# A 3x3 convolution in column tiles: four products of 32 channels, one for each strip of seven image columns

## The chip, the cores and the metric

The kernel runs on one core of a Trainium2 chip. The metric is the device time of one execution in microseconds (us). A core has a matrix engine (TensorE, PE in the profile; PEld is its loading of weights), VectorE (DVE), ScalarE (ACT), GpSimd (POOL) and SyncE (SP), which here issues nearly all transfers. [...]

## The reference

The input is 32 images of 56 x 56 positions with 96 channels, fp32. Layer 0 is a block with a convolution:

```python
h = (x - mean) * rsqrt(var + eps) * ln_w + ln_b           # over the 96 channels
x1 = (einsum('bhwc,cd->bhwd', h, w_in) + b_in)[..., :192]
y = conv3x3(x1, conv_w, padding='SAME') + conv_b          # 192 -> 96 channels
x = x + silu(y)
```

Layer 1 takes the 3136 positions of an image as tokens. It adds a token mixer and then a feed-forward part, each after a normalisation over the channels:

```python
h = relu(bn1(einsum('bnc,hc->bnh', ln(t), w1)))           # 96 -> 192
X = fft(h, axis=1, norm='ortho')
xr = relu(X.real * rd - X.imag * id + rb)
xi = relu(X.imag * rd + X.real * id + ib)
t = t + bn2(einsum('bnh,ch->bnc', ifft(xr + 1j * xi).real, w2))
t = t + ffn(ln(t))                                        # 96 -> 384 -> 96, quantized
```

The values in the feed-forward part are rounded to an 8-bit float before each product.

## The kernel before

**Layout.** A token's number is 28 p + j. The partition p has 112 values (56 image rows, two halves of a row), and j is one of 28 columns in a half row. Tiles of tokens are [112, columns, 96]. LN_CHUNKS cuts the 28 columns into chunks of 8, 8, 8 and 4; a *group* g is four columns, and there are seven.

**Convolution.** w_in and the 3x3 weights are folded into one kernel when the program starts. In the direction of the rows it is done in a transformed form: `image` multiplies the normalised tokens (xa) by the table rows6. This gives, for each of 14 groups of four image rows, six sums of rows, with channels on partitions, in the tile img of [97, 2 halves, 30 columns, 6 sums, 14 groups]. There is one img for all images. `make_seam` copies the columns where the halves meet. `conv` then multiplies img with the weights wv: three *parts* with two of the six sums each, and for each sum three column offsets dx. `conv_sums`, `conv_row` and `conv_silu` turn the parts into four image rows (VectorE) and apply SiLU (ScalarE). `to_tokens` transposes the result back into tokens, and `conv_end` (L398) adds x from a tile of its own and starts the statistics of the next normalisation.

Before the change `conv` works on a chunk: a product has 97 input rows, 96 output channels and 2 x 8 x 14 = 224 columns (112 for the last chunk). An image has 4 x 3 x 6 = 72 of them. The profile shows each fp32 product as two passes.

**The token mixer.** `product_a` and `transform_a` (L209, L218) go through a table to the DRAM tile da; `forward` (L233) fetches it as at and makes px. Its third kind of step, u = 2, puts products of 64 columns into partitions 0 to 63 and 64 to 127 of px. `product_w2` and `inverse` (L272, L276, L286) lead to the DRAM tile de, and `transform_out` (L294) takes it back as y to the tokens. `ffn_tokens`, `ffn_in`, `ffn_relu` and `ffn_out` are the feed-forward part. `ffn_add` (L331, L332) writes the sum to a tile o, and `store` sends o to the output.

**Buffers.** Tiles of conv, image and to_tokens share one tag of PSUM with two buffers (tag q). Tokens t have three buffers for each chunk; x has two, o two. The working tiles m, sd and s have two each.

**Order.** The steps are put into a list with a time each: `plan(b)` gives steps of image b times in units of an eighth of an image, shifted by 8 for each image. CONV, FIRST, BACK and FFN are the times at which convolution, mixer, way back and feed-forward part begin. The list is sorted and the steps are called in that order. The framework then orders the instructions of each engine by its own timeline, with this list as priorities (`schedule_with_timeline_sim=True`), so a step's instructions needn't stay together. Steps of up to five images are under way at a time.

Of the kernel before, what the change touches and what calls it, by code (L numbers as in the profile page):

```python
# [38 lines left out]
F32 = mybir.dt.float32  # L39
# [6 lines left out]
C = 96  # L46
# [15 lines left out]
LN_CHUNKS = ((0, 8), (8, 16), (16, 24), (24, 28))  # L62


LN_W, LN_B, CONV_B, B_IN, BN1, BN2, NPAR = 0, 1, 2, 3, 5, 13, 17
# [15 lines left out]
def hybrid_kernel(ctx: ExitStack, tc: tile.TileContext, x, par, spar, w_in, conv_w, w1, w2, fw1, fb1, fw2, fb2, fa, fb, ib, ia, rows6, out):  # L81
# [18 lines left out]
    convb = par_sb[:, CONV_B : CONV_B + 1]  # L100
# [48 lines left out]
    def image(xa, n, b, j0):  # L149

        ps = psq.tile([C + 1, n, 2, WC * WG], F32, tag="q", name=f"im_{b}_{j0}")
        for j in range(n):
            nc.tensor.matmul(ps[:, j], xa[:, j, :], rows6_sb, start=True, stop=True)  # L153
        nc.scalar.copy(img[:, :, j0 + 1 : j0 + 1 + n].rearrange("c h j k g -> c j h (k g)"), ps)

    def conv(s, part, b, i):

        j0, j1 = LN_CHUNKS[i]
        n = j1 - j0
        ps = s[part] = psq.tile([C, 2, 2, n, WG], F32, tag="q", name=f"cv_{b}_{i}_{part}")  # L160
        for at, k in enumerate(PAIRS[part]):
            for dx in range(3):
                cols = img[:, :, j0 + dx : j1 + dx, k, :]
                nc.tensor.matmul(ps[:, at], wv[:, k, dx, :], cols, start=(dx == 0), stop=(dx == 2))  # L164
        if part == 0:
            m = s["m"] = work.tile([C, 2, 2, n, WG], F32, tag="m", name=f"m_{b}_{i}")
            nc.scalar.copy(m, s.pop(0))

    def conv_sums(s, b, i):

        j0, j1 = LN_CHUNKS[i]
        n = j1 - j0
        m, ps = s.pop("m"), s.pop(1)
        sd = s["sd"] = work.tile([C, 2, 2, 2, n, WG], F32, tag="sd", name=f"sd_{b}_{i}")
        nc.vector.tensor_tensor(sd[:, 0], m, ps, ALU.add)
        nc.vector.tensor_tensor(sd[:, 1], m, ps, ALU.subtract)
        s["y"] = work.tile([C, n, WG, 4, 2], F32, tag="s", name=f"s_{b}_{i}")
        conv_row(s, 1, 1, 2.0)
        conv_row(s, 2, 0, 4.0)

    def conv_row(s, r, at, scale):
        row = s["y"][:, :, :, r, :].rearrange("c j g h -> c h j g")
        nc.vector.scalar_tensor_tensor(row, s["sd"][:, at, 1], scale, s["sd"][:, at, 0], ALU.mult, ALU.add)

    def conv_silu(s):

        sd = s["sd"]
        nc.vector.tensor_tensor(sd[:, :, 0], s.pop(2), sd[:, :, 0], ALU.add)
        conv_row(s, 0, 0, 1.0)
        conv_row(s, 3, 1, 8.0)  # L190
        nc.scalar.activation(s["y"], s["y"], AF.Silu, bias=convb)

    def to_tokens(s, b, g):
        pt = psq.tile([N1, G4, C], F32, tag="q", name=f"st_{b}_{g}")
        for j in range(G4):
            nc.tensor.transpose(pt[:, j, :], s[:, j].rearrange("c r i h -> c (r i h)"), ident[:C, :C])  # L196
        return pt
# [131 lines left out]
    def ffn_add(y1, tg, o, b, g):  # L329
        y2 = work.tile([N1, G4, C], F16, tag="y2", name=f"y2_{b}_{g}")  # L330
        nc.vector.tensor_tensor(y2, y1, b2q, ALU.add)  # L331
        nc.vector.tensor_tensor(o, tg, y2, ALU.add)  # L332

    class Image:


        def __init__(self, b):
            self.b = b
            self.tokens = x[b].rearrange("(p j) c -> p j c", j=N2)
            self.result = out[b].rearrange("(p j) c -> p j c", j=N2)  # L340
            self.x, self.t, self.s, self.n2t, self.hq = {}, {}, {}, {}, {}
            self.u, self.at, self.gt, self.gw, self.held = {}, {}, {}, {}, {}
            self.xa, self.xc, self.rs, self.xl, self.y, self.norm = {}, {}, {}, {}, {}, {}

        def load(self, i):
            j0, j1 = LN_CHUNKS[i]
            self.t[i] = tpool.tile([N1, j1 - j0, C + 1], F32, tag=f"t{i}", name=f"t_{self.b}_{i}")
            self.x[i] = xpool.tile([N1, j1 - j0, C], F32, tag="x", name=f"x_{self.b}_{i}")
            nc.sync.dma_start(self.x[i], self.tokens[:, j0:j1, :])

        def group(self, g, tiles=None):
            return (tiles or self.t)[g // 2][:, g % 2 * G4 : (g % 2 + 1) * G4, :]
# [21 lines left out]
    def make_image(im, i, j, n):  # L374
        image(im.xa[i][:, j : j + n], n, im.b, LN_CHUNKS[i][0] + j)

# [5 lines left out]
    def conv_part(im, i, part):  # L382
        if part == 0:
            im.s[i] = {}
        conv(im.s[i], part, im.b, i)

    def conv_first(im, i):
        conv_sums(im.s[i], im.b, i)

    def conv_last(im, i):  # L390
        conv_silu(im.s[i])

    def conv_tokens(im, g):
        im.held["st", g] = to_tokens(im.s[g // 2]["y"][:, g % 2 * G4 :], im.b, g)

    def conv_end(im, g):

        nc.vector.tensor_tensor(im.group(g)[:, :, :C], im.held.pop(("st", g)), im.group(g, im.x), ALU.add)  # L398
        for i in ended(g):
            im.rs[i] = stats(im.t[i], "b", im.b, i)  # L400

    def deviation(im, i):

        _, var, rs = im.rs[i]
        nc.vector.tensor_tensor(im.t[i][:, :, C], var, rs, ALU.mult)
# [65 lines left out]
    def back_end(im, g):  # L471

        tg = im.group(g)[:, :, :C]
        nc.vector.tensor_tensor(tg, im.held.pop(("py", g)), tg, ALU.add)
        for i in ended(g):
            mu, _, rs = stats(im.t[i], "c", im.b, i)
            im.norm[i] = mu, None, rs

    def normal(im, g, j):

        i = g // 2
        if j == 0:
            im.xc[g] = xnp.tile([N1, G4, C], F32, tag="xn", name=f"xn_{im.b}_{g}")
        mu, _, rs = im.norm[i]
        xc = im.xc[g]
        for j in (j, j + 1):
            at = g % 2 * G4 + j
            nc.vector.tensor_scalar(xc[:, j], im.t[i][:, at, :C], mu[:, at : at + 1], rs[:, at : at + 1], ALU.subtract, ALU.mult)  # L488
# [15 lines left out]
    def ffn_end(im, g):  # L504
        o = im.held["o", g] = work.tile([N1, G4, C], F32, tag="o", name=f"o_{im.b}_{g}")
        ffn_add(im.held.pop(("y1", g)), im.group(g)[:, :, :C], o, im.b, g)

    def store(im, g):
        o = im.held.pop(("o", g))
        nc.sync.dma_start(im.result[:, g * G4 : (g + 1) * G4, :], o)  # L510
# [8 lines left out]
    def plan(b):  # L519
# [5 lines left out]
        for i, (j0, j1) in enumerate(LN_CHUNKS):  # L525
            last = i == len(LN_CHUNKS) - 1

            at = CONV - 8 + 2 * (i + 1)
            ats = (-0.95, -0.7) if last else (0.2, 0.5, 0.85) if i == 2 else (0.25, 1.0, 1.5)
            put(at + ats[0] - (2.5 if b else 12), fetch, i)  # L530
            put(at + ats[0] - 1.15, take_in, i)
            for part, j in enumerate(range(0, j1 - j0, 3)):
                put(at + ats[part], make_image, i, j, min(3, j1 - j0 - j))

            at = CONV + 2 * i
            put(at + 0.6, im_load, i)
            ats = (0, 0.35, 0.7) if last else (0, 0.5, 1.25)
            for part in range(3):
                put(at + ats[part], conv_part, i, part)
            put(at + ats[1] + 0.2, conv_first, i)  # L540
            put(at + ats[2] + 0.2, conv_last, i)
            for g, off in zip(range(j0 // G4, j1 // G4), (1.85, 2.75)):
                put(at + off, conv_tokens, g)
                put(at + off + 0.15, conv_end, g)
            put(FIRST + 2 * i - 0.75, deviation, i)
        put(CONV - 0.6, make_seam)
# [23 lines left out]
        for m, (p0, p1) in enumerate(UNITS):  # L570
            both = p1 - p0 > PG
            for at, u in ((0, 0), (0.62, 1), (1.25, 2)) if both else ((0, 0), (0.62, 2)):
                at += 2 * m
                put(at, second, m, u)
                put(at + 0.22, second_parts, m, u)
                put(at + 0.42, second_relus, m, u)
# [6 lines left out]
    def im_load(im, i):  # L583
        im.load(i)

    CONV, FIRST, BACK, FFN = -12.3, -8, 8.38, 10.85
# [14 lines left out]
    run(CONV - 0.1)  # L601

    with tc.tile_pool(name="setup", bufs=1) as sp, tc.tile_pool(
# [4 lines left out]
        nc.sync.dma_start(spar_sb, spar)  # L608
        win = sp.tile([C, H], F32, name="win")
# [118 lines left out]
    tpool = ctx.enter_context(tc.tile_pool(name="tpool", bufs=3))  # L728
    xpool = ctx.enter_context(tc.tile_pool(name="xpool", bufs=2))
# [8 lines left out]
def dft_tables():  # L738
# [58 lines left out]
    for g in range(WG):  # L797
        for i in range(6):
            r = 4 * g + i - 1
            if 0 <= r < HW:  # L800
                for h in range(2):
                    rows6[r, h, h, :, g] = sums[:, i]
    tables = fa.reshape(N1, 112), fb.reshape(112, -1), ib.reshape(114, NP, 112), ia, rows6.reshape(N1, -1)
# [48 lines left out]
```

## Time and profile before

| | |
|---|---|
| median of 3 runs | 3285.62 us (3276.33 to 3288.96) |
| profiled execution | 3286.24 us, its span 3284.5 us |
| busy: PE, PEld, DVE, ACT, POOL | 3178.5, 2732.7, 2527.3, 2202.5, 573.4 us |
| chain that ended last | PE 88%, DMA 7%, DVE 2% |
| convolution's passes (L164) | 4608, 22% of the chain |
| granted TensorE clock, mean | 0.985 |
| transfers | 355.45 MB in 334551 packets, 129304 of them under 512 bytes; main queue 37.7% of 16 engines |

The span is the time from the first instruction to the last. Busy shares are unions of instruction times[...]. The chain is followed back from the last instruction to what released it. An image takes some 102 us in the middle of the span.

### The profile page before, as it was taken

How to read it: one execution, taken by the hardware profiler on the slowest of the kernel's cores; microseconds unless marked ns; L12 is line 12 of the kernel's file. 1: busy time of each engine (PE TensorE's matmuls, PEld its weight loads, DVE VectorE, ACT ScalarE, POOL GpSimd, SP SyncE). 2: the span in 40 equal slices, each digit the busy share in tenths (PEclk: the TensorE clock that was granted, in tenths of full speed). 3: DMA queues.
4: the chain of work that ended last, by engine and by line, in shares of the span. 5: the costliest groups of instructions: out<-in, count | busy, mean ns of one | idle time of the engine just before them, and what ended most of it. 6: DMA issues, size and time to landing. Idle time of an engine off the chain costs nothing.

```text
span 3284.5 us, 66741 instructions
## 1 busy us (share of the span) xinstructions
PE 3178.5 (97%) x23701; PEld 2732.7 (83%) x23701; DVE 2527.3 (77%) x7829; ACT 2202.5 (67%) x5232; POOL 573.4 (17%) x397
## 2 busy tenths in 40 slices
PE   7999999999999999999999999999999999999997
PEld 6888888888888888888888888888888888888875
DVE  4558777777878777877877777777777778777787
ACT  2566666766766666766666766667767666666776
POOL 1211111111211111112111111111111111121111
PEclk8999999999999999999999999999999999999997
DMA  4343334434344333344333344343344333443341
GB/s 109 94 116 98 104 110 123 120 99 112 94 118 120 109 107 105 106 117 119 111 102 109 107 117 123 96 112 104 110 123 119 100 103 101 120 118 99 104 117 55
DMA packets 334551, 355.45 MB, mean 108 GB/s; under 512 B 129304, under 2 KB 287400, under 8 KB 333992
## 3 DMA queue, kind: packets, MB, share of 16 engines
q1 hardware_dynamic: 332210, 349.01, 37.7%
q8 instruction: 188, 3.08, 0.4%
q10 hardware_dynamic: 2008, 2.17, 0.2%
q14 instruction: 145, 1.19, 0.1%
HBM read 196.93 MB, written 154.14 MB: 107 GB/s over the span
## 4 chain that ended last, share of the span: by engine, by line
PE 88%; DMA 7%; DVE 2%; ACT 1%; issue 1%; SPq 1%; POOL 0%; ACTq 0%; DVEq 0%; POOLq 0%
PE cv L164 22%; PE px L233 9%; PE pa L218 9%; PE ph L209 9%; PE im L153 7%; PE pg L276 5%; PE pe L286 5%; PE tp_n L146 5%; PE pg L272 5%; PE py L294 5%; PE pf L305 4%; PE po L322 3%; DMA de<-es 2%; PE st L196 2%; DMA at<-da 2%; DMA y<-de 1%
## 5 line engine op out<-in xcount | busy, mean ns | idle before, releaser
L164 PE MATMUL cv<-img,wv 97*96 97x224 f32 (+1 forms) x4608 | 882.4, 332 | 0.2
L164 PEld LDWEIGHTS cv<-img,wv 97*96 97x96 f32 x4608 | 662.0, 164 | 93.2 <-issue 11.2
L138 POOL TENSOR_TENSOR rs_c<-var_c,mhalf 112x8 f32<-112x8 f32 (+1 forms) x128 | 195.0, 1523 | 1679.7 <-DVE var_a L136 868.9
L212 ACT ACTIVATE h<-ph,rs_b 112x192 f32<-112x192 f32 x896 | 332.3, 429 | 177.5 <-PE ph L209 176.2
L233 PEld LDWEIGHTS px<-fb_sb,at 112*64 112x64 f32 (+1 forms) x3584 | 324.7, 165 | 132.7 <-issue 48.9
L233 PE MATMUL px<-fb_sb,at 112*64 112x112 f32 (+3 forms) x3584 | 381.9, 274 | 35.1 <-DMA at<-da 34.1
L307 ACT CAST h<-pf 128x448 f16<-128x448 f32 x672 | 363.8, 541 | 67.8 <-PE pf L305 64.5
L209 PE MATMUL ph<-w1a,n2t 97*112 97x192 f32 x1792 | 373.7, 328 | 4.1 <-DVE sv L252 2.8
L218 PE MATMUL pa<-h,fa_sb 112*112 112x384 f32 x896 | 365.6, 490 | 0.0
L138 POOL TENSOR_TENSOR rs_b<-var_b,mhalf 112x8 f32<-112x8 f32 (+1 forms) x128 | 190.4, 1488 | 984.7 <-DVE var_a L136 552.1
L153 PE MATMUL im<-rows_sb,xa 112*97 112x168 f32 x1792 | 325.2, 312 | 11.0 <-DVE xa L372 9.8
L488 DVE TENSOR_SCALAR xn<-t,st_c,rs_c 112x96 f32<-112x96 f32 x896 | 232.2, 325 | 111.3 <-POOL rs_c L138 108.7
L249 DVE SCALAR_TENSOR_TENSOR sv<-px,spar_sb,av 128x224 f32<-128x224 f32 (+2 forms) x352 | 153.4, 436 | 200.2 <-ACT av L240 199.3
L209 PEld LDWEIGHTS ph<-w1a,n2t 97*112 97x112 f32 x1792 | 290.7, 177 | 17.4 <-DVE sv L252 3.3
L153 PEld LDWEIGHTS im<-rows_sb,xa 112*97 112x97 f32 x1792 | 268.0, 167 | 43.2 <-issue 14.7
L219 ACT COPY u<-pa 112x384 f32<-112x384 f32 x448 | 215.4, 481 | 120.8 <-PE pa L218 111.5
L316 DVE CAST hq<-h 128x448 fp8e5<-128x448 f16 x672 | 257.9, 384 | 11.3 <-ACT h L313 5.4
L315 DVE TENSOR_SCALAR h<-h,b1q 128x448 f16<-128x448 f16 x658 | 215.4, 327 | 59.2 <-ACT h L307 54.4
L305 PE MATMUL pf<-n3t,w1q 96*128 96x448 fp8e5 x672 | 243.8, 363 | 9.6 <-ACT h L307 8.8
L276 PE MATMUL pg<-w2x,gt 128*112 128x96 f32 (+1 forms) x1792 | 251.6, 261 | 0.0
L238 ACT ACTIVATE av<-px,spar_sb 128x224 f32<-128x224 f32 (+2 forms) x352 | 156.7, 445 | 135.3 <-PE px L233 132.5
L276 PEld LDWEIGHTS pg<-w2x,gt 128*112 128x112 f32 (+1 forms) x1792 | 242.7, 179 | 0.2
(115 smaller groups left out, 6148.1 us busy)
## 6 DMA issues: line engine op xcount, KB each, us to landing
da<-u SPq DMA_DIRECT2D x224, 336.0 KB, 3.4
at<-da SPq DMA_DIRECT2D x224, 336.0 KB, 4.7
de<-es SPq DMA_DIRECT2D x448, 84.0 KB, 2.2
y<-de SPq DMA_DIRECT2D x224, 168.0 KB, 2.8
out<-o SPq DMA_DIRECT2D x224, 168.0 KB, 2.4
xl<-in_x SPq DMA_DIRECT2D x96, 336.0 KB, 3.4
x<-in_x SPq DMA_DIRECT2D x96, 336.0 KB, 4.1
xl<-in_x SPq DMA_DIRECT2D x32, 168.0 KB, 2.3
```

The source lines that it names most:

```text
L138: nc.gpsimd.tensor_tensor(rs, var, mhalf[:, :n], ALU.pow)
L153: nc.tensor.matmul(ps[:, j], xa[:, j, :], rows6_sb, start=True, stop=True)
L164: nc.tensor.matmul(ps[:, at], wv[:, k, dx, :], cols, start=(dx == 0), stop=(dx == 2))
L209: nc.tensor.matmul(ph[:, j, :], n2t[:, 2 * j2 + j, :], w1a, start=True, stop=True)
L212: nc.scalar.activation(h[:, j], ph[:, j], AF.Relu, scale=rs[:, 2 * j2 + j : 2 * j2 + j + 1])
L218: nc.tensor.matmul(pa, fa_sb, h, start=True, stop=True)
L233: nc.tensor.matmul(px[rows, j], lhs, fb_sb[:, first(p) : first(p + 1)], start=True, stop=True)
L276: nc.tensor.matmul(pg[:, half, j, :], lhs, w2x, start=False, stop=True, skip_group_check=True)
L305: nc.tensor.matmul(pf, w1q[:, k * 128 : (k + 1) * 128], n3t, start=True, stop=True)
L307: nc.scalar.copy(h1, pf)
L316: nc.vector.tensor_copy(hq[:, k, :], h2, saturate=False)
L488: nc.vector.tensor_scalar(xc[:, j], im.t[i][:, at, :C], mu[:, at : at + 1], rs[:, at : at + 1], ALU.subtract, ALU.mult)
```

## The change

The convolution is cut by output channels and by columns instead of by chunks:

- Output channels come in three blocks r of 32 (NR, CB). The 28 columns come in four strips t of seven (NT, CT). For each block, part, sum and dx there are four products with 32 output channels and 2 x 7 x 14 = 196 columns, one for each strip. Their results lie in partitions 32 t to 32 t + 31 of one PSUM tile, so an image has 3 x 3 x 6 x 4 = 216 products, in nine parts of 24.
- The steps after the products work on [128, ...] tiles with 392 elements, three times an image instead of four.
- A transpose in `to_tokens` now turns a [128 = 4 strips x 32 channels, 112] piece, and gives one column of each strip. So tokens are held in ORDER (0, 7, 14, 21, 1, 8, ...): the input, the tables and the output are permuted to match outside the timed program.
- The convolution of a block needs all columns. `make_image` takes two columns at a time. All of the next image's columns are planned after the last part of this image, where before chunks of both alternated.
- x is loaded into t itself, in two halves of 16 and 12 columns (HALVES), and the convolution's result is added in place. The statistics of the next normalisation become a step of their own, `norm_b`. `ffn_add` adds in place too, and the output is stored from t. Tiles x and o are gone, and t has four buffers.
- CONV goes from -12.3 to -14.7 and BACK from 8.38 to 8.5; the first px of an image is planned 0.14 units later.

```diff
+NT, CT = 4, N2 // 4
+CB, NR = 32, 3
+HALVES = ((0, 4), (4, NG))
+ORDER = [CT * t + g for g in range(NG) for t in range(NT)]
...
-    def image(xa, n, b, j0):
-        ps = psq.tile([C + 1, n, 2, WC * WG], F32, tag="q", name=f"im_{b}_{j0}")
-        for j in range(n):
+    def image(xa, b, g, t0):
+        ps = psq.tile([C + 1, 2, 2, WC * WG], F32, tag="q", name=f"im_{b}_{g}_{t0}")
+        for j in range(2):
             nc.tensor.matmul(ps[:, j], xa[:, j, :], rows6_sb, start=True, stop=True)
-        nc.scalar.copy(img[:, :, j0 + 1 : j0 + 1 + n].rearrange("c h j k g -> c j h (k g)"), ps)
+        j0 = CT * t0 + g + 1
+        nc.scalar.copy(img[:, :, j0 : j0 + CT + 1 : CT].rearrange("c h j k g -> c j h (k g)"), ps)
...
-        ps = s[part] = psq.tile([C, 2, 2, n, WG], F32, tag="q", name=f"cv_{b}_{i}_{part}")
+        ps = s[part] = psq.tile([128, 2, 2, CT, WG], F32, tag="q", name=f"cv_{b}_{r}_{part}")
         for at, k in enumerate(PAIRS[part]):
             for dx in range(3):
-                cols = img[:, :, j0 + dx : j1 + dx, k, :]
-                nc.tensor.matmul(ps[:, at], wv[:, k, dx, :], cols, start=(dx == 0), stop=(dx == 2))
+                for t in range(NT):
+                    cols = img[:, :, CT * t + dx : CT * (t + 1) + dx, k, :]
+                    w = wv[:, k, dx, r * CB : (r + 1) * CB]
+                    nc.tensor.matmul(ps[t * CB : (t + 1) * CB, at], w, cols, start=(dx == 0), stop=(dx == 2))
...
-    def to_tokens(s, b, g):
-        pt = psq.tile([N1, G4, C], F32, tag="q", name=f"st_{b}_{g}")
-        for j in range(G4):
-            nc.tensor.transpose(pt[:, j, :], s[:, j].rearrange("c r i h -> c (r i h)"), ident[:C, :C])
+    def to_tokens(s, b, r, half):
+        g0, g1 = HALVES[half]
+        pt = psq.tile([N1, g1 - g0, 128], F32, tag="q", name=f"st_{b}_{r}_{half}")
+        for g in range(g0, g1):
+            nc.tensor.transpose(pt[:, g - g0, :], s[:, g].rearrange("c r i h -> c (r i h)"), ident)
...
-        nc.vector.tensor_tensor(o, tg, y2, ALU.add)
+        nc.vector.tensor_tensor(tg, tg, y2, ALU.add)
...
+        def load(self, half):
+            n = G4 * (HALVES[half][1] - HALVES[half][0])
+            self.t[half] = tpool.tile([N1, n, C + 1], F32, tag=f"t{half}", name=f"t_{self.b}_{half}")
+            j0 = G4 * HALVES[half][0]
+            nc.sync.dma_start(self.t[half][:, :, :C], self.tokens[:, j0 : j0 + n, :])
...
+    def conv_end(im, r, half):
+        t = im.t[half][:, :, r * CB : (r + 1) * CB]
+        st = im.held.pop(("st", r, half)).rearrange("p j (t c) -> p (j t) c", c=CB)
+        nc.vector.tensor_tensor(t, st, t, ALU.add)
+    def norm_b(im, i):
+        im.rs[i] = stats(im.chunk(i), "b", im.b, i)
...
-        nc.sync.dma_start(im.result[:, g * G4 : (g + 1) * G4, :], o)
+        nc.sync.dma_start(im.result[:, g * G4 : (g + 1) * G4, :], im.group(g)[:, :, :C])
...
+            at = CONV - 2.45 + 0.7 * i
+            put(at - (2.8 if b else 12), fetch, i)
+            put(at - 0.55, take_in, i)
+            for j in range(0, j1 - j0, 2):
+                put(at + 0.08 * j, make_image, i, j)
+            put(CONV + 5.7 + 1.5 * i, norm_b, i)
+            put(FIRST + 2 * i - 0.6, deviation, i)
+        put(CONV - 0.1, make_seam)
+        put(CONV, load, 0)
+        put(CONV + 1.25, load, 1)
+        for r in range(NR):
+            at = CONV + 1.85 * r
+            for part, when in enumerate((0, 0.5, 1.1)):
+                put(at + when, conv_part, r, part)
+            put(at + 0.72, conv_first, r)
+            put(at + 1.32, conv_last, r)
+            for half in range(2):
+                put(at + 1.72 + 0.23 * half, conv_tokens, r, half)
+                put(at + 1.87 + 0.23 * half, conv_end, r, half)
...
-                at += 2 * m
+                at += 2 * m + (0.14 if m + u == 0 else 0)
...
-    CONV, FIRST, BACK, FFN = -12.3, -8, 8.38, 10.85
+    CONV, FIRST, BACK, FFN = -14.7, -8, 8.5, 10.85
...
-    tpool = ctx.enter_context(tc.tile_pool(name="tpool", bufs=3))
-    xpool = ctx.enter_context(tc.tile_pool(name="xpool", bufs=2))
+    tpool = ctx.enter_context(tc.tile_pool(name="tpool", bufs=4))
```

## The prediction

> **What bounds the kernel now.** I read the page's busy shares first, then the chain, then the costliest groups.
>
> ```profile
> PE 3178.5 (97%) x23701; PEld 2732.7 (83%) x23701; DVE 2527.3 (77%) x7829; ACT 2202.5 (67%) x5232; POOL 573.4 (17%) x397
> PE 88%; DMA 7%; DVE 2%; ACT 1%; issue 1%; SPq 1%; POOL 0%; ACTq 0%; DVEq 0%; POOLq 0%
> L164 PE MATMUL cv<-img,wv 97*96 97x224 f32 (+1 forms) x4608 | 882.4, 332 | 0.2
> L233 PE MATMUL px<-fb_sb,at 112*64 112x112 f32 (+3 forms) x3584 | 381.9, 274 | 35.1 <-DMA at<-da 34.1
> ```
>
> TensorE carries 88% of the chain and sits idle 0.2 us before the convolution's passes, so its queue of passes is the time. Busy time overstates it, because passes overlap; what counts is the distance between starts. That comes from the timeline of TensorE (start, length, what, how many):
>
> ```profile
> 1013.64 0.49 PE L209 MATMUL ph<-w1a,n2t 97*112 97x192 f32 x2
> 1013.97 2.06 PE L164 MATMUL cv<-img,wv 97*96 97x224 f32 x10
> 1015.86 0.49 PE L196 MATMUL st<-ident,s 96*112 96x96 f32 x4
> ...
> 1025.62 0.81 PE L218 MATMUL pa<-h,fa_sb 112*112 112x384 f32 x2
> 1026.36 1.01 PE L233 MATMUL px<-fb_sb,at 112*64 112x114 f32 x16
> 1027.30 0.36 PE L305 MATMUL pf<-n3t,w1q 96*128 96x448 fp8e5 x1
> ```
>
> Ten passes of 224 columns take 1015.86 - 1013.97 = 1.89 us, 0.189 each. The trace gives 0.096 for the 112-column form, so a pass costs 0.0027 us plus 0.00083 a column. Each fp32 product is two passes (4608 passes for 72 x 32 products). The convolution is 3456 x 0.189 + 1152 x 0.096 = 764 us, 23.9 us an image; the chain's 22% for L164 (722 us) agrees.
>
> The last three lines are the one place where this kernel already puts products side by side: two of 64 columns into partitions 0 and 64. Sixteen passes of 114 columns, 0.0975 apart if alone, would take 1.56 us. They take about half: their starts come in pairs 0.007 us apart, a pair every 0.097. But the visit is not free. From the first pa to pf are 1.68 us; two pa take 0.65, eight pairs 0.78; 0.25 is left. Over all 164 such visits the median is 0.245, within 0.01 for most of them, and 0.29 if the late weight load of the following product is counted too.
>
> [...] Four tiles at once no line here shows.
>
> **The change part by part.** A unit of the plan is an eighth of an image, 102/8 = 12.75 us.
>
> *Convolution products.* Removed: 72 products an image. Added: 216, of 196 columns and 32 output channels, in 54 groups of four. If a group's four run together, it costs two slots of 0.0027 + 196 x 0.00083 = 0.166 us. So 54 x 2 x 0.166 = 17.9 us an image instead of 23.9: 6.0 saved, 192 in all. All of it lies on the path.
>
> *Mode changes.* A visit to 32-column mode costs what one to 64-column mode does, less some weight load: I take 0.27, ends 0.18 and 0.33. How many visits? The nine parts are at least nine. But the framework's scheduler breaks parts: the trace has 655 runs of cv passes for 384 parts, 1.7 a part, and the timeline of 1200 to 1302 us shows 22 lines of cv for one image. A break also cuts a group of four three times in four, which costs another pair of slots: 0.33 x 3/4 = 0.25. So n visits cost 17.9 + 0.27n + 0.25(n - 9):
> - 9 visits: 20.3 us, -3.6 an image, -115 in all
> - 12: 21.9, -2.0, -64
> - 16: 24.0, nothing
> - 21 (as many as now): 26.6, +2.7, +86
>
> I take 12. The parts are now 9 instead of 12, planned 0.5 units apart at least, and the 64-column visits, which are as coherent as the new ones should be, are broken only 164/128 = 1.3 times a unit. 9 x 1.3 = 12.
>
> *Transposes.* 28 of 96 columns at 0.082 (2.30 us) become 21 of 128 at 0.109: 2.29. Nothing.
>
> *VectorE.* By shape (rows of 448 and 224 elements interpolated to 392, and 224 and 112 to 196): six sums of 0.551, twelve rows of 0.511, three of 0.559, six additions to t of 0.689 or 0.552: 14.8 us an image, now 17.7 (442 + 124 over 32). That is -2.9. *ScalarE.* im copies are 14 of 0.451 instead of 11 mixed ones, m and SiLU are 3 instead of 4: 10.7 us, now 11.6. Both engines lie beside TensorE, so nothing is counted. The in-place addition has the shape of the former one (551 ns).
>
> *Transfers.* x goes into t, with 97 elements to a column, and the output leaves from it: runs of 384 bytes instead of 3072 and 1536. The trace's packets take 24, 173 and 79 ns (means). Loads go from 2.15 to 2.42 ms of one engine, stores from 1.99 to 2.42: +44 us on 16 engines over the span, from 37.7% to 39%[...]. Hidden behind TensorE. SP issues two loads an image fewer. A load of t's second half waits for the store four images back, planned 0.2 units (2.5 us) before; a store takes 2.4 us to land. So SP may stand up to 2.4 us an image, with at<-da and y<-de behind it. I count nothing, at most +50 us.
>
> *Moved starts.* The first px of an image is planned 0.14 units later and the way back 0.12: 1.8 and 1.5 us. What they meet, in the view of the waits (us, times, longest):
>
> ```profile
> PEld px L233 <- DMA at<-da: 45.8, 32, 3.0
> ...
> PE px L233 <- DMA at<-da: 34.1, 32, 2.5
> ...
> PE py L294 <- DMA y<-de: 15.6, 18, 2.5
> ```
>
> Once an image TensorE waits some 1.1 us for at and half of that for y. The later start covers most. I take -30 us, ends 0 and -50.
>
> *New waits.* Convolution, which was spread over the image, now lies in 5 of 8 units, and building the next image in the other 2.4, since img has one buffer. Statistics and scaling for the next image (9 us of VectorE) fall into 2.3 units (28 us), where its other work is 14 + 2: 89% busy, against 79% in the present windows. Behind a late xa on TensorE stand im and all that follows. The present excess over the bare distances between starts is 4.4 us an image, mode changes and the waits above in it. I take +25 us, ends 0 and +110.
>
> *Filling.* Conv starts 2.4 units earlier and a first image's tokens wait for all three channel blocks: +5 us, ends 0 and 20.
>
> Sum: -64 - 30 + 25 + 5 = -64. The profiled execution took 3286.2 (span 3284.5 and 1.7 around it), the median of the runs is 3285.6, so the reference is the same. **3222 us.** About 0.5%, 16 us, is what a measurement can tell.
>
> **The rivals.**
> 1. *Broken stretches: slower.* If the scheduler breaks the parts as often as now an image, 21 visits: +86 instead of -64, so 3286 + 86 - 30 + 25 + 5 = 3372. It decides from 17 visits on, with the other terms as taken. For it: 1.7 runs a part now, and a part is four times as many instructions. Against it: the 64-column visits hold together.
> 2. *New waits as long as the gain.* [...] if VectorE or SP comes late by 3 us an image beyond what I counted, the sum is +32: 3318. For it: 89% in one window. Against it: VectorE and ScalarE lose 3.8 us of work an image.
> 3. *Fewer than four at once.* [...] only two run together: 54 x 4 x 0.166 = 35.8 us, +17.9 an image over the case of four: about 3795. Milder: a pass every 0.052 us, the spacing of the fp8 passes in L322, the densest single-tile row here, against 0.041 needed: 432 x 0.052 = 22.5 us, +147, so 3369. Against both: pairs at 0.007, and 0.049 a pass in px.
> 4. *Nothing to see.* With 16 visits and the other terms as taken the sum is 0; a visit more or less is 0.52 us an image, 17 in all.
>
> **How the numbers follow.** Forecast 0.52 (3150 to 3269), rival 4 0.10, rival 1 0.17, rival 2 0.11, rival 3 0.10 (half of it beyond 3450). Slower is 0.38. The range 3150 to 3390 leaves out 0.05 below and some 0.13 above. Faster and slower both hold much; the forecast's own range is 3150 to 3269.
>
> **What would show it.** Right: cv passes in groups of four starts within 0.03 us, slots 0.166 apart, 432 passes an image in about 22 us, some 12 runs of cv an image; VectorE's busy time down by some 90 us, ScalarE's by 30; the wait for at under 20 us; DMA share near 39%. Wrong: over 16 runs an image, gaps of 0.33 between slots inside a run, or more than 1 us an image of new waits for xa, the sums or at. The forecast fails if the sum of such gaps exceeds 2 us an image.

## The result, and the profile after

The changed kernel takes 3543.53 us (median of 4 runs, 3539.41 to 3549.83), the kernel before 3284.72 in the same job (3276.33 to 3288.96): **1.0793 times as long, 95% interval 1.0765 to 1.0821**. The forecast was 3222 us, with a range from 3150 to 3390. The profiled execution took 3549.83, its span 3548.0, 263.5 more than the span before.

The page of the changed kernel: busy shares, chain, the main DMA queue and the groups that answer to those shown of before (after the second bar: idle time just before them, and what ended it):

```profile
PE 3355.8 (95%) x32693; PEld 2550.8 (72%) x32693; DVE 2468.7 (70%) x7573; ACT 2192.7 (62%) x5264; POOL 611.6 (17%) x397
...
q1 hardware_dynamic: 492610, 349.01, 38.0%
...
PE 88%; DMA 6%; ACT 4%; DVE 1%; issue 0%; SPq 0%; ACTq 0%; DVEq 0%
...
L171 PE MATMUL cv<-img,wv 97*32 97x196 f32 x13824 | 818.7, 338 | 0.8 <-DVE wv L654 0.4
L171 PEld LDWEIGHTS cv<-img,wv 97*32 97x32 f32 x13824 | 433.1, 110 | 311.4 <-issue 158.9
...
L240 PE MATMUL px<-fb_sb,at 112*64 112x112 f32 (+3 forms) x3584 | 396.7, 282 | 94.1 <-DMA at<-da 94.1
...
L225 PE MATMUL pa<-h,fa_sb 112*112 112x384 f32 x896 | 386.6, 514 | 33.0 <-ACT h L219 33.0
```

The main thing is what has not moved. TensorE is still the bound. VectorE and ScalarE have less to do than before (2468.7 against 2527.3, 2192.7 against 2202.5), and DMA is at 38%. The convolution's busy time went from 882.4 to 818.7 us only, though groups of four in two slots each (a slot is the distance from one set of parallel passes to the next) would need 573 us between starts, instead of 764. And px waits for at 94 us instead of 34, while pa now waits for h, which it did not do before.

The timeline of TensorE (start, length, line and tile, how many passes) shows why the convolution didn't get shorter. One part is 24 products, 48 passes:

```profile
1501.61 0.53 PE L171 MATMUL cv<-img,wv 97*32 97x196 f32 x6
1502.08 0.36 PE L312 MATMUL pf<-n3t,w1q 96*128 96x448 fp8e5 x1
1502.37 0.86 PE L171 MATMUL cv<-img,wv 97*32 97x196 f32 x14
1503.16 0.90 PE L225 MATMUL pa<-h,fa_sb 112*112 112x384 f32 x2
1503.90 0.81 PE L301 MATMUL py<-y,ia_sb 113*112 113x384 f32 x2
1504.64 1.52 PE L171 MATMUL cv<-img,wv 97*32 97x196 f32 x28
```

6 + 14 + 28 are the 48 passes of one part, in three visits. Six passes are three products, so the first group of four is cut: three strips run, the fourth comes 0.76 us later. From the start of that pf to the next cv pass are 0.29 us, though a full pf lasts, start to start, 0.19.

A *visit* is a stretch of cv passes in 32-column mode (products of 32 output channels in partitions 32 t to 32 t + 31) with nothing else between them. Taken over the whole trace: the groups do run as four at once (starts of a group 0.007 us apart, groups' slots 0.166 us apart, as forecast), but there are **723 visits, 22.6 an image, instead of the 12 of the forecast**, and 3988 slots instead of 54 x 2 x 32 = 3456. The difference, 532 slots, comes from groups that are cut. In the median 0.093 us are lost before a visit's first pass and about 0.10 behind its last one. Its first slot and the first step behind it are longer than usual, too: 0.191 us instead of 0.166, and by some 0.09 us.

The trace lets the whole difference be counted. Take the distance from each TensorE pass to the next, and subtract the usual distance of a pass of that form; what is left is nearly all idle time, lies at a visit, or falls where the record of the granted clock says one half. From the kernel before to the changed one this gives, over the whole spans:

| | us |
|---|---|
| streaming of the convolution, no group cut | -190 |
| 532 extra slots | +88 |
| visits: steps at changes of mode and inside visits +150, the step behind a visit +46 | +196 |
| TensorE idle (90 us became 177) | +86 |
| steps at half clock (41 us became 124 beyond the usual distances) | +83 |

These make +263 of the 263.5 us; what all other steps add and save cancels. A visit costs 196 / 723 = 0.27 us. Of the changes between cv passes and other full-width passes in the kernel before, 1298 steps, the same count gives 4 us in all.

The second place is the wait for at. Same view of the changed kernel, around the first px of an image (in brackets: idle before it, and what ended it):

```profile
1524.55 0.81 PE L225 MATMUL pa<-h,fa_sb 112*112 112x384 f32 x2
...
1529.18 0.21 PE L329 MATMUL po<-w2q,hq 128*112 128x96 fp8e5 x1
1532.43 1.95 PE L240 MATMUL px<-fb_sb,at 112*128 112x114 f32 x8 [3.04 <-DMA at<-da]
1534.18 0.29 PE L329 MATMUL po<-w2q,hq 128*112 128x96 fp8e5 x1
...
1546.01 1.04 PE L240 MATMUL px<-fb_sb,at 112*128 112x114 f32 x8
```

and in the kernel before:

```profile
1499.27 0.81 PE L218 MATMUL pa<-h,fa_sb 112*112 112x384 f32 x2
...
1502.25 2.44 PE L164 MATMUL cv<-img,wv 97*96 97x224 f32 x12
...
1507.33 0.58 PE L164 MATMUL cv<-img,wv 97*96 97x224 f32 x2
1508.74 1.15 PE L233 MATMUL px<-fb_sb,at 112*128 112x114 f32 x8 [0.82 <-DMA at<-da]
```

Between the last pa of an image and its first px lies a round trip through DRAM: u is stored to da and fetched as at. The chain that ended last has both (start, length):

```profile
1525.93 2.82 DMA da<-u
...
1528.83 3.56 DMA at<-da
```

Before, convolution passes lay in that gap: 14 of them, some 2.6 us. In the changed plan that part of the image belongs to im, the convolution is over, and nothing takes their place. Read the two px lines of the changed kernel against each other as well: the same eight passes take 1.95 us behind the wait and 1.04 us 14 us later. TensorE's clock had been lowered: its record is at one half from 1532.6 to 1536.0. In the kernel before, with 0.82 us of wait, they take 1.15.

### The profile page after: what moved, and what is told of

Read it like the earlier page. It is cut to its first block, busy times and chain, and to the rows that moved or that the text cites. A ratio compares the mean times of both kernels' runs of the same rounds, so it can differ in the third digit from the quotient of the medians.

```text
span 3548.0 us, 83912 instructions
## 1 busy us (share of the span) xinstructions
PE 3355.8 (95%) x32693; PEld 2550.8 (72%) x32693; DVE 2468.7 (70%) x7573; ACT 2192.7 (62%) x5264; POOL 611.6 (17%) x397
## 4 chain that ended last, share of the span: by engine, by line
PE 88%; DMA 6%; ACT 4%; DVE 1%; issue 0%; SPq 0%; ACTq 0%; DVEq 0%
PE cv L171 22%; PE px L240 10%; PE pa L225 9%; PE ph L216 8%; PE im L158 6%; PE tp_n L151 6%; PE pe L293 5%; PE pg L283 4%; PE pg L279 4%; PE py L301 4%; PE po L329 4%; PE pf L312 4%; DMA at<-da 3%; PE st L203 3%; DMA da<-u 2%; ACT img L160 1%
## 5 line engine op out<-in xcount | busy, mean ns | idle before, releaser
L171 PE MATMUL cv<-img,wv 97*32 97x196 f32 x13824 | 818.7, 338 | 0.8 <-DVE wv L654 0.4
L171 PEld LDWEIGHTS cv<-img,wv 97*32 97x32 f32 x13824 | 433.1, 110 | 311.4 <-issue 158.9
L240 PE MATMUL px<-fb_sb,at 112*64 112x112 f32 (+3 forms) x3584 | 396.7, 282 | 94.1 <-DMA at<-da 94.1
L240 PEld LDWEIGHTS px<-fb_sb,at 112*64 112x64 f32 (+1 forms) x3584 | 345.7, 173 | 193.0 <-DMA at<-da 102.5
L225 PE MATMUL pa<-h,fa_sb 112*112 112x384 f32 x896 | 386.6, 514 | 33.0 <-ACT h L219 33.0
L158 PE MATMUL im<-rows_sb,xa 112*97 112x168 f32 x1792 | 341.3, 330 | 11.2 <-DVE xa L384 9.6
L158 PEld LDWEIGHTS im<-rows_sb,xa 112*97 112x97 f32 x1792 | 293.0, 181 | 27.8 <-DVE xa L384 9.6
L143 POOL TENSOR_TENSOR rs_b<-var_b,mhalf 112x8 f32<-112x8 f32 (+1 forms) x128 | 203.1, 1597 | 303.4 <-DVE var_a L141 297.4
L413 DVE TENSOR_TENSOR t<-st,t 112x512 f32<-112x512 f32 x192 | 118.9, 619 | 184.3 <-PE st L203 180.0
L329 PEld LDWEIGHTS <-hq 128*112 128x112 fp8e5 x2688 | 204.8, 139 | 52.2 <-DVE hq L323 19.7
```

Source lines behind the costliest of these rows:

```text
L143: nc.gpsimd.tensor_tensor(rs, var, mhalf[:, :n], ALU.pow)
L171: nc.tensor.matmul(ps[t * CB : (t + 1) * CB, at], w, cols, start=(dx == 0), stop=(dx == 2))
L225: nc.tensor.matmul(pa, fa_sb, h, start=True, stop=True)
L240: nc.tensor.matmul(px[rows, j], lhs, fb_sb[:, first(p) : first(p + 1)], start=True, stop=True)
L329: nc.tensor.matmul(po[:, j, :], hq[:, k, j * N1 : (j + 1) * N1], w2q[:, k, :], start=(k == 0), stop=(k == 2))
```

## The experiments

Theory A: the breaks (visits and cut groups) cost what the gain was and more. Rival B: the plan does, with the convolution pressed into five of eight units and waits at its seams; breaks are only its visible side. Rival 3 of the prediction, that fewer than four tiles run at once, is refuted by the starts above.

**1. A part's products one after another.** Each product but a part's first is ordered behind the one before it and raised in priority, so nothing comes in between. Nothing else is changed.

```
+        lead = None
...
+                    with ExitStack() as whole:
+                        if lead is not None:
+                            whole.enter_context(tc.issue_after(lead))
+                            whole.enter_context(tc.high_priority(3000))
+                        mm = nc.tensor.matmul(...)
+                        lead = mm.ins
```

> The changed kernel with the 24 products of a part issued one after the other, nothing between them: 267 visits to 32-column mode instead of 723, and no group of four cut. Theory A (mode visits and cut groups are the loss): the trace after has 0.256 us of overhead a visit, some 0.045 more for the late weight load behind it, and 3988 slots where 3456 are enough; 456 x 0.30 + 532 x 0.166 = 225 us less, so about 3320 us. Theory B (new waits of the new plan are the loss): the visits only filled time in which TensorE would wait, so less than 110 us is gained and the time stays over 3430.

Measured: 3257.85 us, ratio to before 0.9946 (0.9929 to 0.9963), 286 less than the changed kernel. 267 visits, 3456 slots. The page and the timeline:

```profile
L176 PE MATMUL cv<-img,wv 97*32 97x196 f32 x13824 | 639.6, 334 | 0.5 <-DVE wv L660 0.4
...
L246 PE MATMUL px<-fb_sb,at 112*64 112x112 f32 (+3 forms) x3584 | 371.3, 275 | 38.5 <-DMA at<-da 37.9 <-PE ph L222 0.2 <-DVE t L496 0.2
```
```profile
1520.14 4.19 PE L176 MATMUL cv<-img,wv 97*32 97x196 f32 x96
```

The 96 passes of two parts stand in one visit of 4.19 us: 23 distances of 0.166 and the full length of the last passes, 0.33; what a visit costs lies before and behind it (0.093 and about 0.10 us in the changed kernel). A is right, and the gain is more than the count of visits and slots gave: the wait for at fell from 94 to 38 us too, and that for h from 33 to 13.

**2. Only the groups of four kept together.** As 1, with `lead = None` set anew for each dx, so that a part may be broken between groups but not inside one.

> The changed kernel with only the four products of a group kept together; parts may still be broken between groups: 695 visits instead of 723, but 3456 slots instead of 3988. Theory A: 28 x 0.30 + 532 x 0.166 = 96 us less than the changed kernel, about 3450 us. If cut groups cost nothing (the other tiles of a cut slot were filled by something else), within 20 us of the changed kernel's 3543. Theory B: also near 3543.

Measured: 3449.75 us, 1.053 (1.0514 to 1.0545). Visits are 695, slots 3456, and the wait for at stays:

```profile
PE px L246 <- DMA at<-da: 89.8, 32, 3.3
```

So the cut groups cost 94 us, against 532 x 0.166 = 88. Between this kernel and 1 lie 192 us for 428 visits, 0.45 each, more than the 0.27 of a visit: of the rest, 24 us are less idle time and 61 us less loss at half clock, counted as above.

**3. One full-width product in place of the four.** The plan, the tiles and all later steps of the change stay, but a group of four is one product of 128 weight columns over the first strip. The convolution is not computed.

```
-                for t in range(NT):
-                    ...
+                cols = img[:, :, dx : CT + dx, k, :]
+                w = wv[:, k].rearrange("c d o -> c (d o)")[:, r * CB : r * CB + 128]
+                nc.tensor.matmul(ps[:, at], w, cols, ...)
```

> The changed kernel in all its plan and its transfers, but each group of four products of 32 channels replaced by one product of 128 columns of weights over the first strip (so the convolution's values are not computed: strips 1 to 3 are left out and the weights are not those of one block). As many slots as an ideal group needs, 108 an image, but no 32-column mode. Theory A: the convolution falls from some 880 us (846 in and around its passes, 33 of late loads) to 573, so about 3236 us, below the kernel before. Theory B: the waits stay, and the breaks make room for them; over 3350.

Measured: 3251.98 us, 0.9929 (0.9913 to 0.9945). The page:

```profile
L170 PE MATMUL cv<-img,wv 97*128 97x196 f32 x3456 | 672.0, 334 | 1.2 <-ACT m L173 0.8 <-DVE wv L653 0.4
...
L239 PE MATMUL px<-fb_sb,at 112*64 112x112 f32 (+3 forms) x3584 | 386.4, 277 | 74.6 <-DMA at<-da 73.7 <-DVE t L489 0.8
```

With no 32-column mode and no group to cut, 292 us of the difference to the changed kernel are gone, near A's number. But B has a share: 573 us of passes instead of 764 gained only 24 us on the kernel before in the same job. The wait for at is 74 us here without any 32-column mode, so most of it belongs to the plan.

**4. The kernel before with the data movement of the change.** x is loaded into t, the sums are made in place, the output leaves from t; convolution and plan are as before.

```
-            nc.sync.dma_start(self.x[i], self.tokens[:, j0:j1, :])
+            nc.sync.dma_start(self.t[i][:, :, :C], self.tokens[:, j0:j1, :])
...
-        ffn_add(im.held.pop(("y1", g)), im.group(g)[:, :, :C], o, im.b, g)
+        ffn_add(im.held.pop(("y1", g)), im.group(g)[:, :, :C], im.group(g)[:, :, :C], im.b, g)
```

> The kernel before with only the movement of data changed: x loaded into t (runs of 384 bytes), the convolution's result and the feed-forward result added in place, the output stored from t, four buffers of t for the first three chunks. Theories A and B: TensorE's queue hides it, 3285 us within 0.5%. Rival C (small runs and the wait of a load for the store of the same buffer lengthen the transfers TensorE waits for): 40 us or more slower, with longer waits for at and y.

Measured: 3239.34 us, 0.9888 (0.9872 to 0.9903): faster by 37 us, not the same. Its waits:

```profile
PE px L233 <- DMA at<-da: 8.1, 8, 2.8
...
PE py L294 <- DMA y<-de: 4.8, 8, 1.4
```

34 and 15.6 us of waiting became 8 and 5, 37 us less together; the time at half clock (see kernel 13 below) went from 20 us to none. The queue share of DMA rose to 40.5%, so smaller transfers did not hurt.

**5 to 7. The price of one visit.** 5 is 1 with one tiny full-width fp8 product (one column) put into the middle of each part, which makes two visits of one. 6 is the kernel before with its parts kept together in the way of 1. 7 is 6 with the same tiny product.

```
+            if at == 0:
+                with tc.issue_after(lead), tc.high_priority(3000):
+                    mm = nc.tensor.matmul(ps_all[:, 511:512], w1q[:, :128], w1q[:, :1], ...)
+                    lead = mm.ins
```

> The kernel of e1 (parts whole, 3258 us) with one tiny fp8 product of 128 weight columns and one moving column in the middle of each part, whose result nothing reads: the same order otherwise, 555 visits to 32-column mode instead of 267, no group cut. Theory A: 288 x (0.30 + 0.03 for the product itself) = 95 us more, about 3353. If a visit costs only what waits happen to stand beside it (theory B), 288 x 0.03 = 9 us more, about 3267.

> The kernel before with the six products of a part issued one after the other: 383 runs of cv instead of 655, all in 128-column mode. Theory A: a break without a mode change costs nothing, so the same as before within 0.5%. If breaks as such cost (weights loaded late at each change of work), some 272 x 0.05 to 0.3 = 14 to 80 us less than before.

> The kernel of e6 with the tiny product of e5 in the middle of each of its 384 parts: there is no mode change here. Theory A: only the product itself, 384 x 0.03 = 12 us more than e6. If the tiny product costs as much here as in e5 (theory B: it is the change of work, not of mode), 384 x 0.33 = 127 us more.

Measured: 5 took 3344.46 us (1.0206, 1.0186 to 1.0227), 86.6 more than 1 for 288 more breaks, 0.30 each. 6 took 3277.55 (1.0002, 0.9995 to 1.0009): 381 runs of cv passes instead of 655, and no difference. 7 took 3295.86 (1.0068, 1.0047 to 1.0089), 18.3 more for 384 tiny products, 0.048 each. The wait for at fell to 9 us in 6 without a gain, so the time of 6 alone would be weak evidence; but the 4 us for 1298 steps, counted above, say the same. So a break costs next to nothing by itself, the tiny product 0.05, and **leaving 32-column mode and coming back 0.25 us**. That is the size forecast from the 64-column visits (0.27, from 0.245 measured there).

**8. The first px later.** 1 with the first px of an image planned at 0.4 instead of 0.14 units.

> The kernel of e1 with the first px of an image planned 0.4 units after its time instead of 0.14 (266 visits). In e1 TensorE waits 37.9 us for at there. If that wait is a matter of the place in the order, most of it goes and the time falls by 20 to 35 us to about 3230; if the transfers as such are late (SP's queue behind a store), it only moves and the time stays within 10 us of 3258.

Measured: 3268.89 us, 0.9976 (0.9961 to 0.999), 11 us more than 1. The waits:

```profile
PE py L307 <- DMA y<-de: 22.5, 21, 2.1
...
PE px L246 <- DMA at<-da: 11.2, 16, 3.3
```

The wait for at fell from 38 to 11 us, but that for y, the second round trip, rose from 10 to 22. TensorE's idle time is 151 us in all, against 145 in 1: the wait only changed its place.

**9. How much of a saved pass comes out in the old plan.** 4 with 14 of the 18 products of a chunk: dx = 1 is left out in four of the six sums.

> The kernel of e4 (before's plan, 3239 us) with 14 of the 18 products of each chunk: the middle offset dx = 1 is left out for four of the six sums (so its convolution is not the reference's). The passes fall from 764 to 594 us, nearly the 573 that four tiles at once stream. Theory D (what ate the streaming gain in e3, 3252 us, is the changed plan, convolution in 5 of 8 units, whose waits the old plan doesn't have): some 150 of the 170 us are gained, 3070 to 3110. Theory E (with a shorter convolution the other engines' chains are the bound, whatever the plan): less than half is gained, over 3155.

Measured: 3117.92 us, 0.9495 (0.9471 to 0.952). Against 4, 170 us of passes were taken out, and 121 of them, 71%, came out in the time, between the two numbers expected. The comparable kernel under the plan of the change is 3, which has the same data movement as 4: with 191 us less of passes it is 13 us slower than 4, so nothing of them came out. TensorE idles 189 us in it against 55 in 4, and loses 83 us at half clock against 30; these 187 us eat it up. So the old plan passes a saving on far better, though not whole: py waits for y 33.5 us there.

**10. Two parts in one visit.** 1 with parts 0 and 1 of a block planned at one time and kept together.

```
+        lead = s.get('lead') if part == 1 else None
...
+        s['lead'] = lead
...
-            for part, when in enumerate((0, 0.5, 1.1)):
+            for part, when in enumerate((0.3, 0.3, 1.1)):
```

> The kernel of e1 with the first two parts of a block planned together and kept together (206 visits to 32-column mode instead of 267). Theory A: 61 x 0.27 = 16 us less than 3258, about 3242, if holding both PSUM buffers of tag q doesn't delay im and st; with such a delay 3260 or more.

Measured: **3228.74 us, 0.9841 (0.9814 to 0.9867)**: 206 visits, and the fastest kernel here that computes the whole convolution. It beats the kernel before by 1.6% and the changed one by 315 us. The gain on 1 is 29 us where 61 visits at 0.25 us are 15; TensorE's idle time fell too, from 145 to 127 us, which was not forecast. Kernel 4, without any column tiles, is at 0.9888: of the 1.6%, the data movement gives 1.1 by itself in the old plan, and what column tiles and the new plan add together is about 0.5.

**11 and 12. The halves of 4.** 11 only loads x into t; 12 only adds the last sum in place and stores from t.

> The kernel before with only x loaded into t, where the convolution's result is added in place (four buffers of t for the first two chunks; the output still goes through the tile o). If the gain of e4 (37 us) is SP's: the load of x no longer stands for one of the two x buffers with the transfers of da and at behind it, so 20 to 37 us less than before. If it is the output's: nothing.

> The kernel before with only the feed-forward sum added in place and stored from t; x still goes through its own tile. If the gain of e4 is the output's, 20 to 37 us less than before; if it is SP's wait for an x buffer, within 0.5% of before.

Measured: 3273.51 (0.9976, 0.9965 to 0.9987) and 3278.94 (0.9986, 0.9978 to 0.9994): 8 and 4 us less than before. The wait for at is 42.5 in one, 5.9 in the other. The two halves don't add up to 37 us, and a shorter wait is not all of it (12 has it, and gains 4 us). Counted from the steps of the traces, 4 has 37 us less idle time than the kernel before and 11 us less loss at half clock. 12 has 26 and 14 less, but pays some 10 at about 100 more changes of mode and 16 in other steps. The order of instructions is new in each of these kernels (630, 703 and 674 runs of cv in 11, 12 and 4, instead of 655); why it falls out so differently stays open.

**13 and 14. The clock after a long wait.** The trace has a record of TensorE's granted clock. Between 100 us after the start and 140 before the end it is at one half for 20 us in the kernel before and for 178 in the changed one. There it has 31 stretches of mostly 3.4 or 6.8 us. The 30 from 240 us on begin between 1.3 us before and 1.6 us after the end of a wait of px of 2.1 to 3.3 us. To see whether that is a cost of its own, extra products that nobody uses are put behind an image's last pa and ahead of its first px, 7 in one kernel and 14 in the other. They fill the wait and leave the outputs as they were.

```
+        if fill is not None:
+            for j in range(7):
+                nc.tensor.matmul(px[:, j % 4], fill[:, 3, :128], fb_sb[:, :2 * w], ...)
```

> The changed kernel with 7 extra products a image (fb_sb against the last u, 14 passes of 114 columns, about 1.4 us), put behind the last pa of an image and ahead of its first px, in the tile that px then overwrites; outputs as before. In the trace of the changed kernel TensorE waits about 3 us there for at, 31 times (94 us), and for 4 to 6 us after a wait of 2.6 us or more the same passes take twice as long (28 such stretches, some 80 us lost, against 16 in the kernel before). Theory H, the half clock after a long wait is real and costs these 60 to 70 us: the extra passes lie inside the wait, which falls below 2 us (px waits about 50 us in all), the slow stretches go, and the kernel with more work is faster: 3475 to 3500. Theory R, the doubled lengths cost nothing (other waits absorb them): 3535 to 3590, no gain, or the extra 43 us on top.

> The same with 14 extra products (28 passes, about 2.8 us an image, 88 us in all), about as long as the wait. Theory H: px waits 10 to 25 us in all, no stretch at half clock after it, 3475 to 3510, about as fast as with 7[...]. Theory R: 3540 to 3600.

Measured: 13 took 3497.93 us (1.0668, 1.0644 to 1.0692), **46 less than the changed kernel with 44 us more of passes** (41 less by the two ratios, as they ran in different jobs). 14 took 3541.22 (1.0796, 1.0772 to 1.082), as much as the changed kernel with 87 us more. The wait of 13, and its timeline at a px:

```profile
PE px L243 <- DMA at<-da: 53.1, 31, 3.0
```
```profile
1499.76 1.81 PE L237 MATMUL px<-fb_sb,u 112*128 112x114 f32 x14
1506.07 1.15 PE L243 MATMUL px<-fb_sb,at 112*128 112x114 f32 x8 [1.44 <-DMA at<-da]
```

The filled 44 us and the remaining wait of 53 are together about the former 94. The clock is at half for 65 us instead of 178, and the eight px passes take 1.15 instead of 1.95 us. Counted from the steps, the span (3548.0 to 3486.7, -61) changed by +50 for passes, -72 for idle time (at -41; the wait of pa for h, 33 us, is no longer among those listed), +23 at 55 more visits and behind them, and -59 at half clock. So the half clock is a real cost, and theory H is right for 7. Why the wait for h went as well is not shown.

For 14 it was wrong by 31 us, and 3541 lies in the range of theory R. Its loss at half clock did fall, from 124 to 46 us in the steps, but px still waits for at 37 us, more than forecast, and new waits arose: pf waits for h 30 us instead of 10 and py for y 18 instead of 1. These, with twice the filling, took back what 13 had gained.

## Why the prediction was wrong, point by point

- *The bound* held: TensorE, by the distance of starts.
- *Four at once* held: 0.007 us inside a group, 0.166 from slot to slot. Rival 3 is refuted by that: its 35.8 us an image took a slot for every two passes.
- *The price of a visit* held: taken 0.27, measured 0.27 by the count of the steps and 0.25 with kernels 5 and 7. That of a slot held as well.
- **The number of visits is the step that failed**: "I take 12", measured 22.6. The argument was a ratio from the 64-column visits of px: those are 8 to 16 passes whose operands come at one time, and they were broken 1.3 times a unit. A part of the convolution is 48 passes, three to six times as long, and nothing in the code keeps the scheduler from putting any other ready product between two of them. What lay nearer was in the prediction, as rival 1: 1.7 runs a part and 22 lines of cv an image in the kernel before. There they cost nothing (kernel 6), and it was this harmless number that had to be carried over, since the same breaks now cost 0.27 us each. The prediction's own sign of being wrong, over 16 runs an image, came true. In the sum, 12 x 0.27 x 32 = +104 became 723 x 0.27 = +196.
- *Cut groups*: taken 0.25 us for three breaks an image, +24 us; measured 532 slots, +88, and 94 by kernel 2. The price of a break was about right: 266 pairs of slots for the 435 visits beyond nine an image are 0.61 pairs a break, where 0.75 were taken. The count again was not.
- *The moved starts*: taken -30, measured +46: at 94.1 instead of 34.1, y 1.3 instead of 15.6. The step looked at when px starts and not at what lay in the round trip before it. The px was planned later by 1.8 us, but 2.6 us of convolution left the gap.
- *New waits*: taken +25. The wait of pa for h alone is 33. What was missed altogether is that a long wait of TensorE costs again behind it: 83 us more are lost at half clock (half of 178 - 20 us in the record is 79). The sums and xa, where I looked for new waits, show none that counts (0.8 us idle before cv, 9.6 for xa, once, as before).
- *Filling*: taken +5, ends 0 and 20. The first px of all starts at 145.6 instead of 132.4 us, 13 later.
- *The engines beside it*: VectorE -59 us instead of -90, ScalarE -10 instead of -30, DMA share 38.0% instead of 39%. None bears on the time. SP's wait of a load for a store, counted at nothing, is 90 us over 56 times in SP's queue; that it sets no end is suggested by the same data movement being faster in kernel 4.

So in place of -64, -30, +25 and +5 stand -190 for streaming, +196 for visits, +88 for cut groups, +86 for idle time (at and y +46 and h +33 of it) and +83 for half clock: +263. Rival 1 named the mechanism, but its 3372 holds the visits and cut groups alone; the waits that came with them, and what they cost at half clock, were not in it. The unit of the plan is 12.45 us rather than 12.75 (an image takes 99.6 us in the middle of the span, from the starts of pa), which changes nothing here.

What the breaks do to the waits is only partly cleared up. The profiled execution of kernel 1 is 294 us shorter than that of the changed kernel. By the steps, 88 of them are cut groups, 128 the 456 visits less, 33 idle time and 63 half clock, less 18 in other steps. So 96 us are waits and what follows them. But the wait for at doesn't come from visits and cut groups alone, since kernel 3 has 74 us of it with neither. That the place of the parts in the order decides is likely, but it was not varied alone.

## What to carry to other kernels

Before products are put side by side in column tiles, count how often the scheduler will break the sequence, from how often it breaks it now, and price each break with a visit (here 0.25 us) and a cut group (here 0.166 us for each further slot). Then keep each group, better a whole part, together by an explicit order, which here turned a loss of 7.9% into a gain of 1.6%. And measure the rest of the change without the column tiles: here that alone gained 1.1%. When work is moved to another part of a plan, look at what it was covering there: here 2.6 us of convolution left the gap between a store to DRAM and the first use of what is fetched, and the wait for at went from 34 to 94 us. And count a wait of TensorE of about 3 us as longer than it is: here the eight px passes behind one of 3.04 us took 1.95 us instead of 1.04.

## What of the hardware was not expected

- **The record showed half the clock behind most waits of 2.6 us or more.** Idle stretches of TensorE were counted over the traces of both kernels and of 1 to 12, between 100 us after the start and 140 before the end. The record had half the clock within 0.8 us of the stretch's end in 69 of 79 cases of 2.6 us or more (only four of the 79 reach 3.4 us; all 28 cases in the changed kernel are among the 69), in 11 of 31 from 2.0 to 2.6 us, and in 14 of 127 from 1.2 to 2.0. The passes agree: in 64 of the 79 cases the next six steps took at least 1.6 times their usual time. The factor is about two (1.95 against 1.04 us for eight px passes), and 30 of the 31 stretches at half clock in the changed kernel begin within 1.6 us of the end of a wait of px.
- Entering and leaving a mode costs the same in 32-column as in 64-column mode (0.25 us by kernels 5 and 7, and 0.245 in the kernel before), and breaking a sequence without a change of mode nothing measurable (kernel 6, 1.0002 of the time before with 381 runs of cv instead of 655, and 4 us for 1298 steps in the kernel before).
- In-place sums, and loads and stores in runs of 384 bytes, raised the share of the DMA queue from 37.7 to 40.5% and made the kernel before faster by 37 us (kernel 4).
